# Holding the first store until eight slots are loaded, and reading the matrices in runs of 16 KB that VectorE sorts

## The chip, the cores and the metric

The kernel runs on one core of a Trainium2 chip. The metric is the device time of that core in microseconds. TensorE does the matrix products, VectorE (DVE) copies, adds and transposes, and the queues of ScalarE (ACT) and SyncE (SP) issue the transfers between HBM and SBUF, which 16 DMA engines carry out. SBUF and PSUM have 128 partitions.

## The reference

Each of 128 samples is a 128 x 1024 matrix in float32. It is multiplied by one of eight 128 x 128 matrices, chosen by the sample's subject number, and added to the product:

```python
def _L0_cond_ref(x, subjects, weights):
    B, C, D, T, N_SUBJECTS = (128, 128, 128, 1024, 8)
    w = weights[subjects]
    out = jnp.einsum('bct,bcd->bdt', x, w)
    return out
x = x + _L0_cond_ref(x, itok_B_0_7, L0_cond_weights)
return x
```

The input x and the output have 67.1 MB each, the eight matrices together 0.52 MB.

## The kernel before

The samples are taken in 32 turns of four (NT = 32, H = 2 halves of G = 2 samples). A turn's four samples lie side by side in one of 12 slots of the tile x_all, 2 MB each, and turn i uses slot i % 12. The result is added into the slot itself and stored from there.

Five instruction streams run beside each other, held together by semaphores that the kernel counts by hand:

- ScalarE's queue issues the loads, four a turn, one for each sample (L199 to L205). The first 12 turns load without waiting; a later turn i waits until the store of turn i - 12 has emptied its slot (L203). A load is a transfer of 32 runs of 16 KB: `transfer` (L50) passes the shape on as written, so that four partitions of 4 KB are filled by each run.
- GpSimd only waits for each turn's loads and passes the word to TensorE through the semaphore s_ready (L207 to L212).
- TensorE runs a loop over the turns (L231). For each half it waits for the matrices (s_go) and for the data (s_ready) and makes four products of N = 512 columns, two for each sample, into the half's part of PSUM (L161).
- VectorE runs a loop over the turns too (L226). For each half it waits for the products, adds PSUM to the slot (L173, one add of 128 x 2048), and copies the next turn's two matrices out of w_all into the operand tiles w0 to w3 (`place`, L152). Before the loop it turns the subject numbers into indices (L194 to L198), waits for the matrices (L222) and places those of turn 0.
- SyncE's queue issues the stores (L214 to L218), each behind a wait for the add that finishes what it stores. Turn 0 is stored in two halves of 1 MB, turns 1 to 30 in one piece of 2 MB, turn 31 in parts. The very last sample's store is L238.

SyncE's queue also reads the subject numbers (L179) and the matrices (L180) at the start. The matrices go with a shape that puts row c of all eight matrices on partition c, so each of the 1024 pieces is one row of 512 bytes.

Of the kernel before, what the change touches and what calls it, by code (L numbers as in the profile page):

```python
# [30 lines left out]
G = 2  # L31
H = 2
# [3 lines left out]
SLOTS = 12  # L36

P_SLOTS = 2

DMA = 16  # L40

IDLE = 3

ROWS = 4

ALIGN = 4096
QUEUES = {mybir.EngineType.SP: "qSPDynamicHW", mybir.EngineType.Activation: "qActDynamicHW"}
# [22 lines left out]
@with_exitstack  # L70
def kernel(
    ctx: ExitStack,
    tc: tile.TileContext,
    x: bass.AP,
    subjects: bass.AP,
    weights: bass.AP,
    out: bass.AP,
):
    nc = tc.nc
    B, C, T = x.shape  # L80
    S, _, D = weights.shape
    NT = B // (G * H)

    def sbuf(name, *shape, dtype=F32):
        return ctx.enter_context(nc.sbuf_tensor(name, list(shape), dtype)).ap()


    room = -(nc.sbuf_base + -nc.sbuf_base % 32) % ALIGN
    if room:
        sbuf("room", C, room // 4)  # L90
    x_all = sbuf("x_all", C, SLOTS * H * G * T)
    xs = [
        x_all[:, i * H * G * T : (i + 1) * H * G * T].rearrange("c (q t) -> c q t", t=T)
        for i in range(SLOTS)
    ]
    w_all = sbuf("w_all", C, S, D)
    ws = [sbuf(f"w{i}", C, 1, D) for i in range(H * G)]
    zeros = sbuf("zeros", C, N)
    given, near, wrap = (sbuf(name, 1, B, dtype=I32) for name in ("given", "near", "wrap"))
    index = sbuf("index", 1, B + H * G, dtype=I32)  # L100
    ps = [
        ctx.enter_context(nc.psum_tensor(f"ps{i}", [D, G, T], F32)).ap() for i in range(P_SLOTS)
    ]

    s_given = tc.alloc_semaphore("s_given")
    s_wall = tc.alloc_semaphore("s_wall")
    s_index = tc.alloc_semaphore("s_index")
    s_zeros = tc.alloc_semaphore("s_zeros")
    s_product = tc.alloc_semaphore("s_product")
    s_added = tc.alloc_semaphore("s_added")  # L110

    s_ready = tc.alloc_semaphore("s_ready")
    s_go = tc.alloc_semaphore("s_go")

    s_slot = [tc.alloc_semaphore(f"s_slot{k}") for k in range(SLOTS)]
    s_head = tc.alloc_semaphore("s_head")
    s_first = tc.alloc_semaphore("s_first")

    def emptied(i):
        turns = i // SLOTS  # L120
        return DMA * (H * G + 1) * turns - (DMA * G if i >= SLOTS and i % SLOTS == 0 else 0)

    def load(engine, i, q):
        transfer(
            nc,
            engine,
            xs[i % SLOTS][:, q, :],
            x[i * H * G + q].rearrange("(a r) t -> a (r t)", r=ROWS),
        ).then_inc(s_head if i * H * G + q < G else s_slot[i % SLOTS], DMA)

    def store(i, q0, q1):
        b = i * H * G
        transfer(
            nc,
            nc.sync,
            out[b + q0 : b + q1].rearrange("g d t -> d g t"),
            xs[i % SLOTS][:, q0:q1, :].rearrange("d (o g) t -> d o (g t)", g=min(G, q1 - q0)),
        ).then_inc(s_first if i == 0 and q1 == G else s_slot[i % SLOTS], DMA)

    def subjects_of(i):  # L140
        _, subject = nc.values_load_multi_w_load_instructions(
            index[0:1, i] if isinstance(i, slice) else index[0:1, bass.ds(i * (H * G), H * G)],
            engines=[mybir.EngineType.DVE],
            min_val=0,
            max_val=S - 1,
            skip_runtime_bounds_check_because="the index is clamped on the chip above",
        )
        return subject

    def place(h, subject):  # L150
        for q in range(h * G, (h + 1) * G):
            copy = nc.vector.tensor_copy(ws[q], w_all[:, bass.ds(subject[q], 1), :])  # L152
        copy.then_inc(s_go, 1)

    def multiply(slot, h):
        nc.tensor.wait_ge(s_go, 1).then_inc(s_go, -1)
        nc.tensor.wait_ge(s_ready, 1).then_inc(s_ready, -1)  # L157
        for q in range(h * G, (h + 1) * G):
            for t in range(0, T, N):
                at = slot * (H * G * T) + (q * T + t)  # L160
                mm = nc.tensor.matmul(  # L161
                    ps[h][:, q % G, t : t + N],
                    ws[q][:, 0, :],
                    x_all[:, bass.ds(at, N)],
                    start=True,
                    stop=True,
                )
        mm.then_inc(s_product, 1)

    def add(slot, h):  # L170
        mine = x_all[:, bass.ds(slot * (H * G * T) + h * G * T, G * T)]
        nc.vector.wait_ge(s_product, 1).then_inc(s_product, -1)  # L172
        nc.vector.tensor_tensor(  # L173
            mine, ps[h].rearrange("d g t -> d (g t)"), mine, ALU.add
        ).then_inc(s_added, 1)

    with tc.tile_critical():  # L177

        nc.sync.dma_start(given, subjects.rearrange("(o b) -> o b", o=1)).then_inc(s_given, DMA)  # L179
        nc.sync.dma_start(w_all, weights.rearrange("s c d -> c s d")).then_inc(s_wall, DMA)  # L180

        nc.vector.memset(zeros, 0.0).then_inc(s_zeros, 1)  # L182
        nc.tensor.wait_ge(s_zeros, 1)
        for _ in range(IDLE):
            nc.tensor.matmul(  # L185
                ps[P_SLOTS - 1][:, G - 1, :N], zeros[:, :D], zeros, start=True, stop=True
            )

        nc.vector.memset(index[:, B:], 0).then_inc(s_index, 1)  # L192
        nc.vector.wait_ge(s_given, DMA)
        nc.vector.tensor_scalar(near, given, -S, S - 1, ALU.max, ALU.min).then_inc(s_index, 1)  # L194
        nc.vector.wait_ge(s_index, 2)
        nc.vector.tensor_scalar(wrap, near, 0, S, ALU.is_lt, ALU.mult).then_inc(s_index, 1)  # L196
        nc.vector.wait_ge(s_index, 3)
        nc.vector.tensor_tensor(index[:, :B], near, wrap, ALU.add).then_inc(s_index, 1)  # L198
        for i in range(NT):  # L199
            if i == SLOTS:  # L200
                nc.scalar.wait_ge(s_first, DMA)
            if i >= SLOTS:
                nc.scalar.wait_ge(s_slot[i % SLOTS], emptied(i))  # L203
            for q in range(H * G):
                load(nc.scalar, i, q)  # L205

        for i in range(NT):  # L207
            if i == 0:
                nc.gpsimd.wait_ge(s_head, DMA * G).then_inc(s_ready, 1)
                nc.gpsimd.wait_ge(s_slot[0], DMA * G).then_inc(s_ready, 1)  # L210
            else:
                nc.gpsimd.wait_ge(s_slot[i % SLOTS], emptied(i) + DMA * H * G).then_inc(s_ready, H)  # L212

        for i in range(NT):  # L214
            for h in range(H):
                if i in (0, NT - 1) or h == H - 1:
                    nc.sync.wait_ge(s_added, i * H + h + 1)
                    store(i, h * G if i in (0, NT - 1) else 0, (h + 1) * G - (i * H + h == NT * H - 1))  # L218


        nc.vector.wait_ge(s_index, 4)
        nc.vector.wait_ge(s_wall, DMA)  # L222
        subject = subjects_of(slice(0, H * G))
        for h in range(H):
            place(h, subject)
        with nc.vector.Fori(0, NT) as turn:  # L226
            subject = subjects_of(turn + 1)
            for h in range(H):
                add(turn % SLOTS, h)
                place(h, subject)  # L230
        with nc.tensor.Fori(0, NT) as turn:  # L231
            for h in range(H):
                multiply(turn % SLOTS, h)

    with tc.tile_critical() as waits:
        for i in range(NT - SLOTS, NT):
            nc.scalar.wait_ge(s_slot[i % SLOTS], emptied(i + SLOTS) + (DMA if i == NT - 1 else 0))
    last = nc.sync.dma_start(out[B - 1], xs[(NT - 1) % SLOTS][:, H * G - 1, :])  # L238

    tc.add_manual_dep(  # L240
        last.ins,
        waits.name,
        mybir.DependencyInfo(mybir.DependencyClass.NoSync, mybir.DependencyReason.SCHED_ONLY),
        reason="the end of the program waits for it",
    )
# [27 lines left out]
```

## Time and profile before

| what | value |
|---|---|
| median of 3 runs | 323.78 us (323.32 to 323.9) |
| the profiled execution | 324.3 us, its span 322.5 us |
| read from HBM / written | 67.63 MB / 67.11 MB |
| mean DMA rate over the span | 418 GB/s |
| products on TensorE (L161) | 232.7 us busy |
| adds on VectorE (L173) | 64, 2291 ns each |
| placing the matrices (L152) | 132 copies, 218 ns each |
| loads of x | 128 of 512 KB, median 31.6 us from issue to landing |
| stores of 2 MB | 30, median 47.1 us from issue to landing |
| the matrices' transfer | 1 of 512 KB, 5.2 us from issue to landing |

The profile's times count from the start of the profiled execution's span. Busy time of an engine says how much of the span it worked; the DMA share is the mean over the 16 DMA engines, and can come out slightly above 1 where packets overlap. A transfer's time from issue to landing contains its wait behind the transfers that were issued before it. The packet records are the trace's list of the single DMA packets, with queue, size, start and length.

### The profile page before, as it was taken

How to read it: one execution, taken by the hardware profiler on the slowest of the kernel's cores; microseconds unless marked ns; L12 is line 12 of the kernel's file. 1: busy time of each engine (PE TensorE's matmuls, PEld its weight loads, DVE VectorE, ACT ScalarE, POOL GpSimd, SP SyncE). 2: the span in 40 equal slices, each digit the busy share in tenths (PEclk: the TensorE clock that was granted, in tenths of full speed). 3: DMA queues.
4: the chain of work that ended last, by engine and by line, in shares of the span. 5: the costliest groups of instructions: out<-in, count | busy, mean ns of one | idle time of the engine just before them, and what ended most of it. 6: DMA issues, size and time to landing. Idle time of an engine off the chain costs nothing. (4 is left out here: it accounts for less than half of the span.)

```text
span 322.5 us, 2381 instructions
## 1 busy us (share of the span) xinstructions
PE 237.1 (74%) x518; PEld 98.1 (30%) x518; DVE 165.7 (51%) x202; POOL 0.2 (0%) x4
## 2 busy tenths in 40 slices
PE   5999998888888888888888888888885995500000
PEld 2434433333333333333333333333331432100000
DVE  2267776666566566666656655666666263600000
POOL 0000000000000000000000000000000000000000
PEclk9799999999999999999999999999999798955555
DMA  7999999999999999999999999999999999999996
GB/s 276 427 391 421 427 428 421 427 429 435 417 427 433 421 425 423 431 427 427 423 424 431 433 419 424 430 426 426 433 426 418 428 425 423 428 429 425 426 425 288
DMA packets 16067, 134.76 MB, mean 418 GB/s; under 512 B 2625, under 2 KB 3650, under 8 KB 3906
## 3 DMA queue, kind: packets, MB, share of 16 engines
q1 hardware_dynamic: 9922, 67.64, 50.0%
q10 hardware_dynamic: 6144, 67.12, 49.5%
q14 instruction: 1, 0.01, 0.0%
HBM read 67.63 MB, written 67.11 MB: 418 GB/s over the span
## 5 line engine op out<-in xcount | busy, mean ns | idle before, releaser
L161 PE MATMUL ps<-x_all,w 128*128 x512 | 232.7, 609 | 39.7 <-PEq L157 39.7
L173 DVE TENSOR_TENSOR x_all<-ps,x_all 128x2048 f32 x64 | 146.6, 2291 | 109.4 <-DVEq L172 109.4
L161 PEld LDWEIGHTS ps<-x_all,w 128*128 128x128 f32 x512 | 96.4, 193 | 176.0 <-issue 175.8
L152 DVE COPY w<-w_all 128x128 f32 x132 | 23.1, 218 | 4.2 <-DMA w_all<-in_L_cond_weights_dram 4.2
L185 PE MATMUL ps<-zeros 128*128 128x512 f32 x6 | 4.4, 890 | 1.7 <-DVE zeros L182 1.7
L185 PEld LDWEIGHTS ps<-zeros 128*128 128x128 f32 x6 | 1.7, 305 | 3.5 <-issue 1.9
L182 DVE MEMSET zeros<- 128x512 f32 x1 | 0.5, 485 | 1.0 <-SPq L177 1.0
L194 DVE TENSOR_SCALAR near<-given 1x128 int32<-1x128 int32 x1 | 0.2, 216 | 0.8 <-DMA given<-in_itok_B_dram 0.8
L198 DVE CUSTOM_DVE_ANT_0 index<-near,wrap 1x256 uint16<-1x256 uint16 x1 | 0.3, 278 | 0.0
L196 DVE TENSOR_SCALAR wrap<-near 1x128 int32<-1x128 int32 x1 | 0.2, 215 | 0.0
L260 POOL MEMSET const-bfloat16-1.0<- 128x1 bf16 x1 | 0.1, 101 | 0.0
L260 POOL MEMSET const-uint8-127<- 128x1 uint8 x1 | 0.1, 101 | 0.0
L260 POOL MEMSET const-float32-0.0<- 128x1 f32 x1 | 0.1, 98 | 0.2 <-issue 0.2
L260 POOL MEMSET const-float32-1.0<- 128x1 f32 x1 | 0.1, 98 | 0.0
L260 DVE BASE_LOAD x1 | 0.0, 15 | 0.1
L192 DVE MEMSET index<- 1x4 int32 x1 | 0.1, 62 | 0.0
## 6 DMA issues: line engine op xcount, KB each, us to landing
x_all<-in_x_dram ACTq DMA_DIRECT2D x128, 512.0 KB, 31.6
out_dram<-x_all SPq DMA_DIRECT2D x30, 2048.0 KB, 47.1
out_dram<-x_all SPq DMA_DIRECT2D x3, 1024.0 KB, 14.4
out_dram<-x_all SPq DMA_DIRECT2D x2, 512.0 KB, 20.6
w_all<-in_L_cond_weights_dram SPq DMA_DIRECT2D x1, 512.0 KB, 5.2
given<-in_itok_B_dram SPq DMA_DIRECT2D x1, 0.5 KB
```

Source lines behind the costliest of these rows:

```text
L152: copy = nc.vector.tensor_copy(ws[q], w_all[:, bass.ds(subject[q], 1), :])
L161: mm = nc.tensor.matmul(ps[h][:, q % G, t : t + N], ws[q][:, 0, :], x_all[:, bass.ds(at, N)], start=True, stop=True,)
L173: nc.vector.tensor_tensor(mine, ps[h].rearrange("d g t -> d (g t)"), mine, ALU.add).then_inc(s_added, 1)
L182: nc.vector.memset(zeros, 0.0).then_inc(s_zeros, 1)
L185: nc.tensor.matmul(ps[P_SLOTS - 1][:, G - 1, :N], zeros[:, :D], zeros, start=True, stop=True)
L192: nc.vector.memset(index[:, B:], 0).then_inc(s_index, 1)
L194: nc.vector.tensor_scalar(near, given, -S, S - 1, ALU.max, ALU.min).then_inc(s_index, 1)
L196: nc.vector.tensor_scalar(wrap, near, 0, S, ALU.is_lt, ALU.mult).then_inc(s_index, 1)
L198: nc.vector.tensor_tensor(index[:, :B], near, wrap, ALU.add).then_inc(s_index, 1)
L260: nc = _bacc.Bacc("TRN2", target_bir_lowering=False, num_devices=1)
```

## The change

The diff has two parts that share one tile.

The matrices are read by `transfer` in memory order: 32 runs of 16 KB, like a sample. Each partition then holds eight rows of one matrix (w_runs), while the products need row c on partition c. VectorE sorts that: one transposition of 128 x 1024 (in blocks of 32 x 32) from w_runs into w_turned, and 16 of 32 x 256 from there back into w_runs. The tile w_turned lies in the last slot of x_all, so ScalarE's queue waits for the last of the 16 before it issues the loads of turn 11. The sorted tile has its columns in blocks of 32 (h, s, l), and `place` copies with that pattern.

Before its loop of stores, SyncE's queue waits until the four loads of slot AHEAD - 1 = 7 have landed. Turn 0 is stored as one piece like the others, and the semaphore s_first, which counted its first half, is gone.

```diff
+AHEAD = 8
+BLOCK = 32
...
-    w_all = sbuf("w_all", C, S, D)
-    ws = [sbuf(f"w{i}", C, 1, D) for i in range(H * G)]
+    RUN = S
+    PER = BLOCK * RUN // C
+    w_runs = sbuf("w_runs", C, S * D)
+    w_all = w_runs.rearrange("c (h s l) -> c h s l", s=S, l=BLOCK)
+    w_turned = x_all[:, (SLOTS - 1) * H * G * T :][:, : S * D]
+    ws = [sbuf(f"w{i}", C, D) for i in range(H * G)]
...
-        ).then_inc(s_first if i == 0 and q1 == G else s_slot[i % SLOTS], DMA)
+        ).then_inc(s_slot[i % SLOTS], DMA)
...
-            copy = nc.vector.tensor_copy(ws[q], w_all[:, bass.ds(subject[q], 1), :])
+            copy = nc.vector.tensor_copy(
+                ws[q].rearrange("c (h o l) -> c h o l", o=1, l=BLOCK),
+                w_all[:, :, bass.ds(subject[q], 1), :],
+            )
...
-        nc.sync.dma_start(w_all, weights.rearrange("s c d -> c s d")).then_inc(s_wall, DMA)
+        transfer(
+            nc,
+            nc.sync,
+            w_runs,
+            weights.rearrange("s c d -> (s c d)").rearrange("(a r) -> a r", r=ROWS * T),
+        ).then_inc(s_wall, DMA)
...
-            if i == SLOTS:
-                nc.scalar.wait_ge(s_first, DMA)
+            if i == SLOTS - 1:
+                nc.scalar.wait_ge(s_wall, DMA + 1 + (C // BLOCK) ** 2)
...
+        nc.sync.wait_ge(s_slot[AHEAD - 1], DMA * H * G)
         for i in range(NT):
             for h in range(H):
-                if i in (0, NT - 1) or h == H - 1:
+                if i == NT - 1 or h == H - 1:
                     nc.sync.wait_ge(s_added, i * H + h + 1)
-                    store(i, h * G if i in (0, NT - 1) else 0, (h + 1) * G - (i * H + h == NT * H - 1))
+                    store(i, h * G if i == NT - 1 else 0, (h + 1) * G - (i * H + h == NT * H - 1))
...
         nc.vector.wait_ge(s_wall, DMA)
+        nc.vector.transpose(w_turned, w_runs).then_inc(s_wall, 1)
+        nc.vector.wait_ge(s_wall, DMA + 1)
+        for a in range(C // BLOCK):
+            for b in range(C // BLOCK):
+                nc.vector.transpose(
+                    w_all[b * BLOCK : (b + 1) * BLOCK, :, a * PER : (a + 1) * PER, :],
+                    w_turned[a * BLOCK : (a + 1) * BLOCK, :].rearrange(
+                        "l (j g b k) -> l b g k j", j=RUN, b=C // BLOCK, k=BLOCK // RUN
+                    )[:, b],
+                ).then_inc(s_wall, 1)
+        nc.vector.wait_ge(s_wall, DMA + 1 + (C // BLOCK) ** 2)
```

## The prediction

> **What bounds the kernel now.** I read the page's slices first, then the kinds of DMA traffic, then the DMA rate in chosen stretches, and last the timelines of the two queues. The slices:
>
> ```profile
> span 322.5 us, 2381 instructions
> PE 237.1 (74%) x518; PEld 98.1 (30%) x518; DVE 165.7 (51%) x202; POOL 0.2 (0%) x4
> ...
> DMA  7999999999999999999999999999999999999996
> GB/s 276 427 391 421 427 428 421 427 429 435 417 427 433 421 425 423 431 427 427 423 424 431 433 419 424 430 426 426 433 426 418 428 425 423 428 429 425 426 425 288
> ```
>
> The DMA engines are busy from the second slice to the last but one, at one rate; TensorE and VectorE are idle for a quarter and a half of the span. The traffic is fixed: 67.63 MB read and 67.11 MB written. Part 4 of the page does not help here, since it follows compute instructions and accounts for about 1% of the span. The question is therefore only where the DMA engines move less than their steady rate. The stretches show that (columns: stretch, length, busy time of each engine, clock, DMA share, GB/s):
>
> ```profile
> 2.00:12.00 10.00, 7.49 (x11) 2.98 (x11) 1.34 (x7) 0.00 (x0) 0.83 1.00 385
> 12.00:17.00 5.00, 5.00 (x13) 1.98 (x11) 2.56 (x3) 0.00 (x0) 1.00 1.00 426
> 14.00:24.00 10.00, 10.00 (x24) 4.08 (x22) 7.68 (x9) 0.00 (x0) 1.00 1.00 397
> 24.00:150.00 126.00, 110.17 (x249) 45.87 (x249) 79.35 (x93) 0.00 (x0) 1.00 1.01 427
> 154.00:268.00 114.00, 94.34 (x208) 39.03 (x208) 68.41 (x79) 0.00 (x0) 0.99 1.01 427
> 272.00:318.00 46.00, 6.50 (x13) 2.44 (x11) 5.12 (x6) 0.00 (x0) 0.57 1.01 426
> ```
>
> Loads alone (12 to 17 us) go at 426 GB/s, both directions at 427, stores alone (272 to 318) at 426. So moving stores later in the program, as such, moves no byte faster or slower. Only two places fall short, although their DMA share is 1.00, that is, packets take longer there rather than being absent: the start, 10 us x (1 - 385/426) = 0.96 us, and the stretch in which the stores begin, 10 us x (1 - 397/426) = 0.68 us. The change touches both.
>
> **Part 1: the matrices' transfer.** Before, L180 reads them as 1024 pieces of 512 bytes. The DMA view of 2 to 12 us gives the engines' time for each queue (q1 is SP's, q10 ScalarE's):
>
> ```profile
> DMA packets 1337, 3.85 MB, mean 385 GB/s; under 512 B 109, under 2 KB 1134, under 8 KB 1134
> ## 3 DMA queue, kind: packets, MB, share of 16 engines
> q10 hardware_dynamic: 295, 3.33, 82.0%
> q1 hardware_dynamic: 1042, 0.52, 17.6%
> ```
>
> The small pieces hold 17.6% of 10 us = 1.76 us of all 16 engines for 0.524 MB. As 32 pieces of 16 KB, which is what every load of x is, the same bytes at 426 GB/s take 1.23 us: 0.53 us saved. The rest of the 0.96 us is 0.43 us: 0.22 us before the first load packet at 2.22 us in the packet records, and some 0.2 us of long packets. By those records 16 KB packets that normally take 0.616 us take up to 1.17 us at the very start and 0.65 to 0.97 us next to the small pieces. The former stay; the latter, estimated at 0.1 us, go. Bounds for this part: 0 (the loss belongs to the start of any stream, not to small pieces) to 0.74 us (all of 0.96 but the 0.22). I take 0.6.
>
> The Trainium skill, "DMA: Bandwidth & Descriptors", section Specifications, speaks against this part: it gives 512 B as the smallest size that goes at line rate, so these pieces should cost what large ones do. This trace disagrees (1.76 us against 1.23); by the page this term would be 0 and the time 323.6.
>
> **Part 2: seventeen transpositions.** No row here shows one. They handle 1024 + 16 x 256 = 5120 elements a partition. At the MEMSET's rate (L182, 485 ns for 512) that is 4.9 us; at the short COPY's (L152, 218 ns for 128) 8.7 us. Taking the copy's 218 ns for the first 128 elements and the MEMSET's 0.95 ns for each further one, 16 x 0.34 + 1.07 = 6.5 us. What waits: VectorE's copies at L152, hence TensorE's first product and the first add. What hides it: the first store no longer needs the first add at once.
>
> ```profile
> 7.41 0.63 DVE L152 COPY w<-w_all 128x128 f32 x4 [4.19 <-DMA w_all<-in_L_cond_weights_dram]
> 14.08 2.29 DVE L173 TENSOR_TENSOR x_all<-ps,x_all 128x2048 f32 x1 [6.04 <-DVEq L172]
> 16.40 3.91 SPq L57 DMA_DIRECT2D out_dram<-x_all  x2
> 26.82 21.77 SPq L57 DMA_DIRECT2D out_dram<-x_all  x4
> ```
>
> The first turn's second add ends at 17.45 + 2.29 = 19.7 us by the timeline; moved by 6.5 us it ends at 26.2. The four stores from 26.82 to 47.99 come 7.06 us apart, TensorE's pace while data is plentiful, so turns 0, 1 and 2 are ready by 40.4. The first store will wait for turn 7's load: 32 loads of 0.524 MB and the matrices, 17.3 MB at 426 GB/s from 2.2 us, with 0.4 us of slow start, about 43 us. The transpositions thus have 17 us of cover and cost nothing; without it they would delay the store stream by up to their 6.5 us, and even then loads would still be filling the DMA engines until turn 11 is in, 25.7 MB, at about 63 us. ScalarE's queue has one wait added, before turn 11's four loads: it reaches them after 44 loads, near 40 us since its queue is full from 15.9 us on and goes at the pace of landing, and the transpositions are done by about 14. Nothing is lost there, although every later load stands behind it.
>
> **Part 3: the first store waits for turn 7.** Behind the wait on SP are all other stores. In the meantime the DMA engines carry loads at the same 426, so no time is lost while it lasts. Afterwards 16 loads (turns 8 to 11, 8.4 MB) are still to land while stores run; at 59% of the engines' time, the loads' share while both run (DMA view of 22 to 150 us), that is some 33 us of cover. Load 12 needs store 0 whole: 2.1 MB at 41.8% of the rate, 12 us, plus about 4 us before its first packet (16.40 to 20.78 in the records for the first store now), so near 59 us. The loads do not run dry. Later they will be bound by free slots from about turn 12 on; before, this begins at turn 22 (ScalarE's issues come in groups of four about 12 us apart from 153.9 us on). The row 154 to 268 above shows that this regime keeps 427 GB/s, so it costs nothing; if each restart of the loads did cost, ten more of them would matter. The tail is the same: the last load still waits for turn 19's store, so the same 22 MB of stores remain behind it, and the queue limits that part, not TensorE.
>
> The start of the stores itself: 0.68 us is lost between 14 and 24 us. The records show why the rate falls: all engines' load packets lengthen from 0.616 to about 1 us between 19.5 and 20.9, just before the first store packet. Either this is what it costs to begin writing beside full loads, and then it moves to 43 us unchanged; or it comes from the meeting of that store with ScalarE's queue, which became full at just that moment (issues of 0.85, 0.91, then 2.45 us from 15.9 on, after 0.62), and then it may vanish, since by 43 us ScalarE has issued nearly all 48 loads. Bounds: 0.68 gained to 1.36 lost (three stores begin together where one of half the size did). I take 0: very long packets also stand at the very start, where ScalarE's queue is not full, so a stream's beginning seems to suffice. One 2 MB store in place of two of 1 MB moves the same bytes: 0.
>
> One more small term: by the records a 16 KB load packet takes 0.612 us when loads run alone and 0.616 beside stores; 10 MB more (610 packets) come alone: 610 x 4 ns / 16 = 0.15 us gained. The rates above do not resolve it; bounds 0 to 0.15, I take 0.15.
>
> **Sum.** The profiled execution took 324.3 us, its span 322.5. 324.3 - 0.6 - 0 - 0 - 0.15 = 323.55. Its runs have a median of 323.78, 0.52 lower, so 323.0 in their terms.
>
> **Rivals.**
> A (forecast): the matrices get cheaper and the stores' beginning costs what it did. 323.0, own range 322.7 to 323.4.
> B: the stores' beginning costs nothing once ScalarE's queue has drained. For it: the coincidence at 15.9 us. Against it: the long packets at 2.2 us. 323.0 - 0.68 = 322.3.
> C: the change does not do what it says at the start: the 0.96 us belong to the stream's beginning, and large pieces save nothing. For it: the long first packets. Against it: the 17.6% of the small pieces. Only 0.15 is left: 323.6. The skill's line-rate rule would end here too.
> D (slower): each store that begins beside a full load queue costs 0.68 us, and three begin at once. For it: nothing in this trace has three stores begin on 16 waiting loads. Against it: the second store, issued at 19.77 us, shows no dip of its own, 24 to 150 us standing at 427. 323.0 + 2 x 0.68 = 324.4. It decides from two extra beginnings on: 1.36 then outweighs the 0.75 gained, one does not.
>
> **How the numbers follow.** A 0.46, B 0.21, C 0.16, D 0.17. The runs before spread by 0.6 us, and about 0.2% (0.65 us) is what a measurement of this kernel can tell from no change; faster thus means below 323.13. A lies just under that line, so 0.58 of it counts as faster (0.27), 0.37 as the same (0.17), the rest (0.02) slower; B is faster (0.21); C the same but for its tails (0.03 faster, 0.11 same, 0.02 slower); D slower, but for 0.03. Sum: faster 0.51, same 0.31, slower 0.18. The range takes in B to most of D: 322.2 to 324.4; A's own is narrower, given above.
>
> **What would show it.** Part 1: in the first 12 us the rate rises from 385 to about 410, SP's queue shows 32 packets more of 16 KB and no 1024 small ones. Part 2: sixteen transpositions near 340 ns, the first add near 20 us, and no store waiting for an add at 43 us. Part 3: loads at 426 to 43 us, 427 afterwards with no dip at slot waits, and a shortfall of 0.68 us near 43 to 48 (A), none (B), or 2 us (D). I am wrong if any stretch after 50 us is below 420, or if the last store is issued while the DMA engines are short of work.

## The result and the profile after

The kernel after takes 324.05 us (median of 22 runs, 323.57 to 324.85), the kernel before 323.59 us in the runs beside it. The ratio is 1.0016, interval 1.001 to 1.0022: about 0.5 us slower, where a gain of 0.75 us, to 323.0 us, was forecast. The direction is wrong. That the time lies inside the stated range is luck: only rival D reached so high, and its price, a loss for each store that begins, is not what was paid.

Mean spans and what of the time lies outside them make it plainer. Over 22 runs the kernel after has a mean span of 322.09 us and 2.03 us outside it; the kernel before, in 33 runs beside the first experiments, 321.83 and 1.78. So about half of the loss lies inside the span and half outside, where the prediction did not look. The profiled execution of before, with a span of 322.5, was one of its longest, so that the two profiled spans, 322.5 and 322.2, suggest a gain that does not exist.

The page of the kernel after:

```profile
span 322.2 us, 2397 instructions
PE 245.1 (76%) x518; PEld 101.2 (31%) x518; DVE 176.5 (55%) x219; POOL 0.2 (0%) x4
...
DMA  7999999999999999999999999999999999999996
GB/s 285 427 429 425 431 409 414 434 425 417 427 439 429 421 415 425 428 429 420 430 423 430 423 432 417 427 431 431 426 418 424 441 415 422 423 429 427 428 424 275
```

The dip of the third slice (391 before) is gone, and a weaker one stands in the sixth and seventh (409 and 414), where the stores now begin. The stretches (columns as before):

```profile
2.00:12.00 10.00, 5.11 (x6) 1.51 (x5) 6.60 (x12) 0.00 (x0) 0.92 1.00 401
12.00:17.00 5.00, 0.00 (x0) 0.00 (x0) 4.75 (x9) 0.00 (x0) 0.50 1.01 429
24.00:43.00 19.00, 19.00 (x44) 7.91 (x43) 12.92 (x16) 0.00 (x0) 1.00 1.01 425
43.00:53.00 10.00, 10.00 (x24) 4.16 (x23) 7.56 (x9) 0.00 (x0) 1.00 1.00 404
53.00:150.00 97.00, 97.00 (x221) 40.65 (x221) 70.35 (x82) 0.00 (x0) 1.00 1.01 426
154.00:268.00 114.00, 97.18 (x196) 39.71 (x194) 62.48 (x75) 0.00 (x0) 0.90 1.01 426
```

The start has 401 in place of 385 GB/s, the stores' beginning 404 in place of 397, and from 24 us on everything else stands at 425 or 426: no later stretch lost its cover. The queues in 2 to 12 us (q1 is SP's):

```profile
q10 hardware_dynamic: 309, 3.49, 86.7%
q1 hardware_dynamic: 48, 0.52, 13.3%
```

The matrices now hold 13.3% of 10 us, 1.33 us of all engines, where the small pieces held 1.76. That 1.76 counts some time twice. In the kernel before, 4 to 5 us is a stretch in which almost nothing but pieces moves:

```profile
DMA packets 664, 0.34 MB, mean 339 GB/s; under 512 B 2, under 2 KB 664, under 8 KB 664
## 3 DMA queue, kind: packets, MB, share of 16 engines
q1 hardware_dynamic: 662, 0.34, 112.1%
q10 hardware_dynamic: 2, 0.00, 0.1%
```

The records of the pieces add up to more than the engines' whole time, although hardly a load packet runs beside them: they overlap one another. What counts is the rate, 339 GB/s here and 315 to 333 in the same stretch of e1_before_again, e2_wait_only and h2_wait_again, three of the runs below. At 339 GB/s the matrices' 0.524 MB take 1.55 us.

VectorE's timeline and the first stores:

```profile
5.86 1.25 DVE L244 STREAM_TRANSPOSE x_all<-w_runs 128x1024 f32<-128x1024 f32 x1 [2.85 <-DMA w_runs<-in_L_cond_weights_dram]
7.14 10.01 DVE L248 STREAM_TRANSPOSE w_runs<-x_all 32x256 f32<-32x256 f32 x16
17.93 0.63 DVE L161 COPY w<-w_runs 128x128 f32 x4 [0.78 <-DVE w_runs L248]
44.25 15.66 SPq L61 DMA_DIRECT2D out_dram<-x_all  x5
```

The sixteen transpositions take 10 us rather than the estimated 5.4, and the first placement comes at 17.93 rather than 7.41 us. The first store goes out when turn 7's last load has landed, at 44.25 us, and does not wait for an add.

Outside the span the trace has something that the page does not print. The DMA view of 322 to 326 us, which is after the span's end, shows one packet in the kernel after and none in an execution of the kernel before:

```profile
DMA packets 1, 0.01 MB, mean 2 GB/s; under 512 B 0, under 2 KB 0, under 8 KB 0
## 3 DMA queue, kind: packets, MB, share of 16 engines
q14 instruction: 1, 0.01, 0.8%
```

It is an instruction fetch of 8 KB, at 324.0 us in the packet records.

### The profile page after: what moved, and what is told of

Same layout as the page of the kernel before. It is cut to its first block, busy times and chain, and to the rows that moved or that the text cites. A ratio compares the mean times of both kernels' runs of the same rounds, so it can differ in the third digit from the quotient of the medians.

```text
span 322.2 us, 2397 instructions
## 1 busy us (share of the span) xinstructions
PE 245.1 (76%) x518; PEld 101.2 (31%) x518; DVE 176.5 (55%) x219; POOL 0.2 (0%) x4
## 5 line engine op out<-in xcount | busy, mean ns | idle before, releaser
L173 PE MATMUL ps<-x_all,w 128*128 x512 | 239.7, 627 | 28.5 <-DVE w L161 14.6
L173 PEld LDWEIGHTS ps<-x_all,w 128*128 128x128 f32 x512 | 99.3, 199 | 169.6 <-issue 168.7
L161 DVE COPY w<-w_runs 128x128 f32 x132 | 23.2, 219 | 0.8 <-DVE w_runs L248 0.8
L248 DVE STREAM_TRANSPOSE w_runs<-x_all 32x256 f32<-32x256 f32 x16 | 9.5, 597 | 0.5
L202 PE MATMUL ps<-zeros 128*128 128x512 f32 x6 | 5.4, 1081 | 1.7 <-DVE zeros L199 1.7
L244 DVE STREAM_TRANSPOSE x_all<-w_runs 128x1024 f32<-128x1024 f32 x1 | 1.2, 1245 | 2.9 <-DMA w_runs<-in_L_cond_weights_dram 2.9
```

Of the source, the lines that this page charges most:

```text
L161: copy = nc.vector.tensor_copy(ws[q].rearrange("c (h o l) -> c h o l", o=1, l=BLOCK), w_all[:, :, bass.ds(subject[q], 1), :],)
L173: mm = nc.tensor.matmul(ps[h][:, q % G, t : t + N], ws[q], x_all[:, bass.ds(at, N)], start=True, stop=True,)
L202: nc.tensor.matmul(ps[P_SLOTS - 1][:, G - 1, :N], zeros[:, :D], zeros, start=True, stop=True)
L244: nc.vector.transpose(w_turned, w_runs).then_inc(s_wall, 1)
L248: nc.vector.transpose(w_all[b * BLOCK : (b + 1) * BLOCK, :, a * PER : (a + 1) * PER, :], w_turned[a * BLOCK : (a + 1) * BLOCK, :].rearrang ...
```

## The experiments

All times are against the kernel before on the same chip, 27 to 33 runs of it in the first four groups and 21 in the last. "Outside" is the mean time less the mean span.

| kernel | what differs from before | ratio, interval | mean span | outside |
|---|---|---|---|---|
| before | | | 321.83 to 321.89 | 1.78 |
| e1_before_again | nothing | 1.0006, 0.9997 to 1.0015 | 321.92 | 1.80 |
| e2_wait_only | wait for turn 7 | 0.9995, 0.9986 to 1.0004 | 321.69 | 1.79 |
| h2_wait_again | the same | 0.9992, 0.9983 to 1.0001 | 321.65 | 1.81 |
| e3_sort_only | runs, transpositions | 1.0022, 1.001 to 1.0033 | 322.44 | 1.92 |
| e4_after_again | all (the kernel after) | 1.0018, 1.0009 to 1.0027 | 322.26 | 2.00 |
| f1_runs_unsorted | wait, runs | 1.0007, 0.9998 to 1.0016 | 322.02 | 1.78 |
| h1_runs_again | the same | 1.0001, 0.9992 to 1.001 | 321.93 | 1.79 |
| g2_runs_4k | wait, pieces of 4 KB | 0.9999, 0.999 to 1.0008 | 321.87 | 1.78 |
| g3_runs_on_act | wait, runs on ScalarE's queue | 1.0009, 1.0 to 1.0018 | 322.20 | 1.79 |
| f2_dead_turns | wait, transpositions for nothing | 1.001, 1.0001 to 1.0019 | 321.93 | 2.06 |
| f3_late_start | wait, first placement at turn 2 | 1.0001, 0.9992 to 1.001 | 321.90 | 1.79 |
| i3_filler6 | wait, 6 MEMSETs | 0.9999, 0.999 to 1.0008 | 321.81 | 1.77 |
| f4_filler | wait, 17 MEMSETs | 1.0009, 1.0 to 1.0018 | 321.83 | 2.03 |
| i4_filler60 | wait, 60 MEMSETs | 1.0002, 0.9993 to 1.0011 | 321.85 | 1.79 |
| j1_after_padded | all, and 43 MEMSETs | 1.0008, 0.9998 to 1.0019 | 322.10 | 1.79 |
| i1_runs_later | wait, runs issued near 19 us | 1.0018, 1.0008 to 1.0028 | 322.50 | 1.77 |
| i2_pieces_later | wait, small pieces near 19 us | 1.0212, 1.0192 to 1.0232 | 328.62 | 1.77 |
| j2_wait11 | wait for turn 11 | 0.9989, 0.998 to 0.9998 | 321.52 | 1.78 |

Each row but the first has 11 runs, i1_runs_later 10 and i2_pieces_later 5. The standard error of a mean span is 0.04 to 0.09 us in most rows, about 0.15 in e3, i1 and j1 and 0.3 in i2, so one difference of 0.1 us between two of these kernels is not resolved.

### Taking the change apart: e1 to e4

e2_wait_only is the kernel before with this edit and with turn 0 stored whole; e3_sort_only is the kernel after without the two:

```diff
-                nc.scalar.wait_ge(s_first, DMA)
...
+        nc.sync.wait_ge(s_slot[AHEAD - 1], DMA * H * G)
```

> The kernel before, unchanged, to see how its executions spread. Theory S (the profiled execution of before was a slow one, 324.3 against a median of 323.59, and its 0.68 us shortfall where the stores begin is not in most executions): a span of about 321.7 and a rate in 14 to 24 us above 410 in this profile. Rival O (the spans are alike, and the kernel after loses outside its span): a span of 322.3 or more, the shortfall again near 0.68 us, and a time less span of about 1.3 us against 2.03 for the kernel after.

> The matrices as before; the first store waits for turn 7 and turn 0 is stored whole. Theory S: the wait costs what the beginning of the stores at 43 us costs more than the one at 16 us, and the matrices' part gains 0.3 to 0.4 us; then this kernel is 0.8 to 0.9 us slower than before. Rival M (the matrices' part costs and the wait is neutral): within 0.1 us of before. Rival O (both are neutral in the span, the extra instructions cost outside it): within 0.1 us of before.

> The matrices in 32 runs with the 17 transpositions; the stores begin as soon as turn 0's first half is added, as before. Theory S: 0.3 to 0.4 us faster than before by the start, unless the later first store (some 10 us later) costs what the wait costs. Rival M: 0.5 us slower than before, like the kernel after. Rival O: 0.5 us slower, with a span shorter than before's.

> The kernel after, beside the others on one chip: 0.5 us slower than before under every theory; its shortfall where the stores begin again near 0.6 us between 43 and 53 us.

Theory S, that the wait costs, fell at once: the wait alone does not lose (mean span 321.69 against 321.83), the sort alone loses 0.6 us inside the span and 0.14 outside. Part of its loss is where its stores begin, at 26.99 us: by the packet records that costs 1.0 us, the most of all these kernels. The dip in before's profile is no accident either; another execution of it has it too (its stretch from 14 to 24 us):

```profile
14.00:24.00 10.00, 9.80 (x23) 3.92 (x23) 6.98 (x10) 0.00 (x0) 1.00 0.98 388
```

What was an accident in the first profiled execution is only that it came out long. Rival M stands for the loss inside the span, where the matrices' part costs, and rival O for the half that lies outside.

### Which half of the matrices' part: f1 to f4

f1_runs_unsorted leaves the 17 transpositions out of the kernel after. f2_dead_turns adds the same transpositions to the wait alone, into a place that nothing reads. f3_late_start and f4_filler add these to the wait alone:

```diff
+        nc.vector.wait_ge(s_slot[2], DMA * H * G)                       # f3_late_start
...
+        for j in range(17):                                              # f4_filler
+            nc.vector.memset(filler[:, 8 * j : 8 * j + 4], 0).then_inc(s_fill, 1)
+        nc.vector.wait_ge(s_fill, 17)
```

> The kernel after without its 17 transpositions and without the wait before turn 11's loads: the matrices come in 32 runs and their rows stay unsorted, so the products are those of other matrices. Theory T (what the sorting program on VectorE costs, late start or longer program, is the whole loss, and the runs gain some 0.1 us): ratio 0.999 to 1.000 to before, time less span 1.8 us, no second instruction fetch. Rival R (the transfer in 32 runs itself is what costs, by leaving one DMA engine later at the end): ratio 1.0015, with time less span 1.8.

> Matrices in 1024 pieces as before, the wait for turn 7, and the same 17 transpositions into a part of slot 11 that nothing reads. Theory T: 0.5 to 0.7 us slower than the kernel with the wait alone (ratio 1.0015 or more to before), time less span 2.0 and an instruction fetch after the span's end. Rival R: within 0.2 us of the kernel with the wait alone in the span.

> The kernel with the wait alone, whose VectorE places the first matrices only when turn 2 has landed, near 17.5 us, as late as in the kernel after; no instruction but one wait is added. If the late start of the products is what costs (by whatever way): ratio about 1.001 and a span of 322.1. If it is the longer program (P): like the wait alone, ratio 0.9995, time less span 1.8.

> The kernel with the wait alone, with 17 small MEMSETs on VectorE where the transpositions stand, about 1 us of work. Theory P (the longer program of VectorE costs, by an instruction fetch): time less span 2.0, a fetch after the span's end as in the kernel after, 0.2 us or more slower than the wait alone. If the late start costs instead: like the wait alone in the span.

Two separate costs come out. Outside the span, the two kernels with 17 more VectorE instructions have 2.06 and 2.03 us, the two without have 1.78 and 1.79. Seventeen MEMSETs, which write 68 words in all and move no data of the kernel, cost outside what seventeen transpositions cost. Of the four, only those two show an instruction fetch after the span's end; f4_filler's, in 322 to 326 us:

```profile
DMA packets 1, 0.01 MB, mean 2 GB/s; under 512 B 0, under 2 KB 0, under 8 KB 0
## 3 DMA queue, kind: packets, MB, share of 16 engines
q14 instruction: 1, 0.01, 0.6%
```

e3_sort_only and e4_after_again have such a fetch too, and no other kernel of the table has one. The line shows in single runs too: each run of a kernel whose profile has the fetch has 1.87 us or more outside, each run of the others, before included, 1.84 or less.

Inside the span, f1_runs_unsorted has 322.02 us without any transposition, against what theory T expected. That is 0.33 more than the wait alone, which ran on another chip, but only 0.1 to 0.2 more than the three kernels with pieces beside it (321.83 to 321.93). A late start of the products is cheap, as predicted: f3_late_start's 321.90 is the mean span of before in the same group.

### The runs against the pieces: h1, h2, g2, g3

h1 and h2 repeat f1 and e2 on one chip. The other two change f1_runs_unsorted:

```diff
-            weights.rearrange("s c d -> (s c d)").rearrange("(a r) -> a r", r=ROWS * T),
+            weights.rearrange("s c d -> (s c d)").rearrange("(a r) -> a r", r=T),     # g2_runs_4k
...
-            nc.sync,
+            nc.scalar,                                                                 # g3_runs_on_act
```

> The same kernel as f1_runs_unsorted (32 runs, unsorted rows, so products of other matrices; the wait for turn 7; no transposition), beside the wait alone on one chip, to settle whether the runs cost or gain inside the span. Theory R2 (the runs save 0.1 us at the start and lose 0.3 us later, where the stores begin and between the DMA engines): mean span 0.2 to 0.4 us above h2_wait_again. Rival Z (the runs are neutral, the difference of 0.2 us so far is chance): mean spans within 0.1 us.

> The same kernel as e2_wait_only: ratio 0.999 to 1.0005 to before, first store issued near 44.7 us, 0.4 us lost where the stores begin, time less span 1.8 us.

> As h1_runs_again, but the matrices in 128 pieces of 4 KB, one for each partition, in the same places (rows unsorted, products of other matrices). If large pieces in a second queue are what costs inside the span (R2), 4 KB pieces lie between: 0 to 0.2 us above h2_wait_again. If the runs are neutral (Z): no difference to either.

> As h1_runs_again, but ScalarE's queue issues the 32 runs ahead of the first load, so that all early traffic is in one queue (rows unsorted, products of other matrices). If the meeting of two queues at the start sets the later loss (R2): 0.2 us or more below h1_runs_again in the span. If not: the same or 0.6 us slower, by the time of one issue, where the first load comes later.

The difference repeated: 321.93 against 321.65, 0.28 us. But the wait alone has the two lowest mean spans of seven kernels with the wait for turn 7 and the pieces at the start; the other five differ from it in VectorE's program alone (f2 also in a wait before turn 11's loads), and the average of the seven is 321.81. Against that average the runs (322.02 and 321.93) cost 0.17 us. What the runs cost inside the span is thus 0.1 to 0.3 us. Pieces of 4 KB, at 321.87, cannot be told from either. On ScalarE's queue the runs are worse (322.20): at 12 us the profiled execution is 3.6 us behind the steady rate by its packet records, where that of h1_runs_again is 2.75 behind. The second half of R2, that one queue would heal the loss, is not borne out.

Where does this time go? The issue of the first store dates the landing of turn 7. It comes at 44.25, 44.89, 44.50, 44.19 and 44.63 us in the five profiles with the wait and runs on SP's queue (after, e4, f1, h1 and, from below, j1), at 44.93, 44.50, 44.74, 44.53, 44.38, 44.62 and 44.89 in seven with pieces (e2, f2, f3, f4, h2 and, from below, i3 and i4): means of 44.49 and 44.66. So the runs do gain at the start, 0.17 us, and lose more than that afterwards. By the packet records (time behind a steady 426.2 GB/s at 46 and 56 us) the stores' beginning costs 0.38 to 0.68 us in the first five and 0.24 to 0.59 in the seven, with means of 0.60 and 0.41. At the very end the last packet ends later than the mean of the 16 DMA engines, by 0.8 us on average in the first five (0.4 to 1.3) against 0.6 in the seven (0.4 to 0.8). These sums go the right way, but five and seven single executions do not show the cause, and it stays open.

### A step or a price for each instruction, and when the matrices may come: i1 to i4

i3_filler6 and i4_filler60 have 6 and 60 in place of f4_filler's 17. The other two hold the matrices' transfer back, the first in f1_runs_unsorted, the second in the wait alone:

```diff
+        nc.sync.wait_ge(s_slot[2], DMA * H * G)
         nc.sync.dma_start(w_all, weights.rearrange("s c d -> c s d")).then_inc(s_wall, DMA)
```

> 32 runs, unsorted (products of other matrices), the wait for turn 7; SyncE issues the runs only when turn 2 has landed, near 17.5 us. If the runs cost by meeting the first loads at the start: mean span within 0.1 us of i2_pieces_later. If they cost by their size (16 engines kept in step, or one left behind) wherever they come: 0.2 to 0.4 us above i2_pieces_later.

> 1024 pieces of 512 bytes as before, the wait for turn 7; SyncE issues the pieces only when turn 2 has landed. If small pieces overlap with loads in full flow better than at the start: 0.2 us below the wait alone, ratio 0.9985 to before. If not: like the wait alone, 0.9993; a late start of the products costs nothing, as f3_late_start showed.

> The wait alone with 6 small MEMSETs on VectorE. If each instruction costs: time less span 1.87 (a third of 0.25 more than 1.78). If it is a step at a fetch boundary: 1.78 without an instruction fetch after the span's end, or 2.03 with one.

> The wait alone with 60 small MEMSETs. If each instruction costs: time less span 2.6. If it is a step: 2.03, as with 17, with one instruction fetch after the span's end.

i3_filler6 came out as a step would have it. i4_filler60 missed, because the step goes down again: with 6 instructions the cost outside is absent (1.77), with 17 present (2.03), with 60 absent (1.79), and then there is no fetch after the span: the packet records of i4_filler60 have one more at 12.2 us instead, where no cost shows. So the price comes with a fetch after the span and not with the number of instructions. That it depends on where VectorE's program ends between two fetches is an inference: no record says what the fetched 8 KB hold.

i2_pieces_later is the instructive miss: 6.8 us slower. Its timeline and its DMA views of 19 to 52 us and, by stretches, of 60 to 80 us:

```profile
53.03 0.63 DVE L153 COPY w<-w_all 128x128 f32 x4 [50.03 <-DMA w_all<-in_L_cond_weights_dram]
```

```profile
w_all<-in_L_cond_weights_dram SPq DMA_DIRECT2D x1, 512.0 KB, 33.0
```

```profile
60.00:70.00 10.00, 10.00 (x24) 4.15 (x23) 7.33 (x9) 0.00 (x0) 1.00 0.72 305
70.00:80.00 10.00, 10.00 (x24) 4.14 (x23) 7.68 (x9) 0.00 (x0) 1.00 0.82 291
```

The 1024 pieces take 33.0 us to land when loads fill the other queue, 5.2 us at the start. Each engine has 64 of them. Their packets stand between 22.9 and 51.2 us in the records, 28.3 / 64 = 0.44 us a piece, and from 24 to 50 us three of them go for every two load packets of 16 KB. The Trainium skill, "DMA: Bandwidth & Descriptors", section "Queues, rings and completion order", says that an engine takes turns between its queues one packet at a time; this trace agrees that they take turns, with 1.5 pieces to a load packet. The products then begin near 54 us, the first store goes out at 65.4, and the DMA engines are short of work between 62 and 76 us. This is the limit of the cover that the prediction counted for the transpositions: loads last until about 63 us, and delay beyond that shows. The runs, issued as late (19.66 us), landed in 7.4 us.

i1_runs_later, at 322.50, is not faster either. Its packet records show that the loss of the start does not need the matrices: with loads alone, packets of up to 1.8 us stand between 4 and 6.5 us, and at 8 us the stream is 3.9 us behind the steady rate. In i2_pieces_later, which begins with loads alone as well, it is 3.3, against 2.6 to 2.9 in the six profiles with the runs in their place on SP's queue and 2.9 to 3.1 in ten with the pieces.

One more thing in it bears on the stores. Their beginning, in 46 to 56 us, first in e2_wait_only, then in i1_runs_later:

```profile
46.00:56.00 10.00, 10.00 (x24) 4.25 (x23) 7.21 (x9) 0.00 (x0) 1.00 0.99 401
46.00:56.00 10.00, 10.00 (x24) 4.09 (x22) 7.68 (x9) 0.00 (x0) 1.00 1.01 424
```

In both, some 15 loads are still to land when the first store is issued, at 44.93 and 45.51 us. By the packet records the beginning costs 0.43 us in the first and 0.01 in the second. The number of loads still queued does not set this cost by itself.

### Two last kernels: j1, j2

j1_after_padded is the kernel after with 43 of the fillers ahead of the transpositions, so that VectorE's program has 60 instructions more than before. j2_wait11 is the wait alone with another number:

```diff
-AHEAD = 8
+AHEAD = 11
```

> The kernel after with 43 small MEMSETs more on VectorE ahead of the transpositions. If the place where the program ends decides: no instruction fetch after the span's end, time less span 1.78 in place of 2.0, and 0.2 us faster than the kernel after, 323.9; the span keeps its 0.3 us over before. If the transpositions themselves cost outside the span: 2.0 and 324.1 to 324.3.

> The wait alone, for turn 11 in place of turn 7 (matrices as before). If the loss where the stores begin comes from beginning beside loads: it shrinks from 0.4 us, and the time is 323.2 or less. If loads run dry before the stores have begun: some DMA engines idle near 63 us, 1 us or more slower.

j1_after_padded has 1.79 us outside, no fetch in 322 to 326 us, and a ratio of 1.0008 where the kernel after had 1.0016 and 1.0018: with more instructions the cost outside is gone. Like i4_filler60 it has one more fetch early on, at 11.4 us. Its span, 322.10, kept the loss inside.

j2_wait11 is the fastest of all, 0.9989 (0.998 to 0.9998), ahead of both kernels, though its interval ends close to 1. Its stretches where the others' stores begin and where its own do:

```profile
43.00:53.00 10.00, 10.00 (x23) 4.02 (x23) 7.22 (x10) 0.00 (x0) 1.00 1.01 426
60.00:70.00 10.00, 10.00 (x24) 4.28 (x23) 6.94 (x10) 0.00 (x0) 1.00 1.01 424
```

Its first store is issued at 59.48 us, when only turn 11's loads are left in the queue, and the beginning costs less than 0.1 us by the packet records in place of 0.63 and 0.66 in the two profiles of before (14 to 24 us). The last loads cover the time to the first store packet, and the DMA engines do not idle.

## Why the prediction was wrong

**Part 1, the matrices: wrong, and the step that failed is the first one, "1.76 us of all 16 engines", from which "0.53 us saved" follows.** The sum of the pieces' packet records was taken as time that nothing else could use. But these records overlap one another (112.1% in 4 to 5 us): at the 339 GB/s of that stretch the matrices took 1.55 us. The runs then took 1.33 us, not the 1.23 of the steady rate. That leaves 0.22 us of the 0.53, and what the first store sees of it is 0.17. The 0.1 us for shorter load packets beside the matrices did not come either: up to 12 us the length of the load packets over 0.611 us each adds up to 0.35 to 0.53 us of all engines in the six profiles with runs and to 0.28 to 0.47 in the ten with pieces. The start loses time with loads alone too (i1_runs_later, i2_pieces_later), and rival C, with 0.16 of the chance, was nearly right for the start: large pieces save little there. The line-rate rule of the Trainium skill ("DMA: Bandwidth & Descriptors", Specifications), which the prediction set aside, gave the nearer term, 0 where 0.17 came and 0.6 was taken, although pieces of 512 B did run below the steady rate in this trace. No bound of this part reached below 0, and that is the second failure: the runs cost 0.1 to 0.3 us inside the span, for a reason that stays open.

**Part 2, the transpositions: right that they are hidden, wrong that they "cost nothing".** They took 11.3 us, not 6.5, the first turn's second add ended at 31 us, not 26, and the first store did not wait. f2_dead_turns and f3_late_start confirm the cover: their mean spans, 321.93 and 321.90, are within 0.1 us of before and of f4_filler on the same chip. But the price of their code was not counted: 0.25 us outside the span, which comes with an instruction fetch that the profile of before could not show and no bound held. This is half of the measured loss.

**Part 3, the wait: right that it costs nothing, but what it gains comes from another place.** Loads alone ran at 425 GB/s, the first store went out at 44.25 us where 43 was worked out, the slot-bound stretch kept 426, and the tail is unchanged. The 0.15 us for shorter load packets did not come: by the packet records packets of loads alone go back to 0.615 us from 18 us on. In its place the stores' beginning became cheaper, 0.41 to 0.60 us on average where before loses 0.63 and 0.66. What the wait gains is 0 to 0.2 us: the mean spans of the wait alone are 0.14 and 0.23 below that of before on the same chip, but neither ratio (0.9995 and 0.9992) is clear of 1, and the five kernels that change VectorE's program besides are between 0.06 below and 0.04 above. The forecast's -0.15 lies within this by luck. Rival B named the right place, and j2_wait11, whose stores begin beside few loads, loses next to nothing there. A full queue on ScalarE as the cause was not tried by itself, though, and i1_runs_later lost nothing there with as many loads to come as the others; what sets this cost stays open. Rival D fell: three stores that begin together cost 0.24 to 0.68 us, no more than the one of before.

**The sum.** All against before on the same chip, and each to about 0.1 us. Inside the span: the wait -0.1, the runs +0.2, and +0.2 more with the transpositions (mean spans of 322.09, 322.26 and 322.10 with them, 322.02 and 321.93 without), near what this can resolve; outside +0.25. Together about +0.5, which is what was measured. The forecast had -0.75.

## What to carry to other kernels

In a kernel whose DMA engines never rest, the engines' time of a small transfer, added up from its packet records, is an upper bound of what removing it saves, since the records can overlap: take the rate of a stretch in which it runs alone, and look for the moment at which the next consumer is released. Here the store stream was best begun when few loads were still queued, while those few covered the way to its first packet; why it is cheaper then is not shown. A change of a few tenths of a microsecond needs the time outside the span in its sum, and a comparison of single profiled executions, which here differ by more than the effect, cannot show it.

## What the hardware showed that was not expected

- Adding instructions to one engine's program can cost in steps. 17 more on VectorE brought an 8 KB instruction fetch after the span and 0.25 us; 6 or 60 more brought neither.
- Pieces of 512 bytes that run alone move at 315 to 339 GB/s, where loads in packets of 16 KB move at 426, and their packet records overlap (112.1% of the engines' time).
- Pieces of 512 bytes queued beside full loads move three for every two 16 KB packets of the other queue: 33.0 us for 0.52 MB.
- A transposition of 32 x 256 float32 with a strided source takes 597 ns, nearly half of the 1245 ns of one of 128 x 1024 that reads in order: 2.3 ns against 1.2 ns for each element of a partition. No run separates the stride from the shorter length.
- The first 8 us of a load stream lose time with loads alone too, and more than with other traffic beside them (3.9 and 3.3 us behind the steady rate in two executions, against 2.6 to 3.1 in sixteen).
